# One block of V combined a slot sooner, two weighted sums a slot later, and the raw weight copies moved to GpSimd, in a masked attention layer on one core

## The chip, the cores and the metric

The kernel runs on one core of one Trainium2 chip. The metric is the device time of one execution in microseconds, lower is better. TensorE is called PE here (its weight loads PEld), VectorE DVE, ScalarE ACT, GpSimd POOL and SyncE SP, as in the profile.

## The reference

128 graphs with 128 nodes of 768 features each, in float32. Twelve heads of 64 features attend over the nodes; the adjacency matrix masks the scores and adds a small bias.

```python
h = jnp.maximum(_layernorm(x, axis=-1), 0.0)
q, k, v = (_split_heads(h @ W + b) for W, b in ((Wq, bq), (Wk, bk), (Wv, bv)))
scores = jnp.einsum('bhqd,bhkd->bhqk', q, k) / jnp.sqrt(HD) + beta * adj_e
scores = jnp.where(adj_e > 0, scores, -9000000000000000.0)
out = jnp.einsum('bhqk,bhkd->bhqd', softmax(scores), v)
return x + out            # heads put side by side again
```

## The kernel before

**Groups and slices.** Four graphs (512 rows) make a group, so there are 32 groups, G = 0 to 31. The projections of a group come in three slices of weight columns: `qk0` (the first half of the columns of Wq and Wk), `v` (all of Wv) and `qk1` (the second half of Wq and Wk), called first, second and third slice. Group 0 is computed plainly (`plain_slice`); while it runs, the weights of the fast scheme below are prepared.

**Products and slots.** From group 1 on, a slice is a matrix product of 3 x 3 blocks worked out by 15 block products in place of 27 (`PRODUCTS`), each of which has again seven inner products in place of eight. One block product is one slot: `product_z` issues 28 matmuls on PE (L540). The left operands are blocks A of the activation and sums S of them (`SUMS_A`, DVE, L454); the right ones are blocks B of the weights and sums T of them, kept in DRAM and loaded again in each group, five ahead (`load_T`, L329), or resident in SBUF. The products add up in PSUM along four chains; `uses` says after which product a chain's value enters which result block (r, j), and with what sign: the first time a copy on ACT or DVE (L553 to L561), later an add on DVE (L564).

**What sets the order.** From group 0's second slice on, the order of instructions is the one written out in the program (`manual_schedule`): each engine works through its instructions in this order, and `todo` lists say in which slot a task is issued. In `run`, a slot issues the matmuls of its product, then `behind_product` (masks of the scores of the slot before, the tasks of this slot, what has been put off until now), then the uses of the product, then the trailing ACT work, then the tasks marked "post". Group 0's first slice stands ahead of that and is ordered by the scheduler of the tile framework.

**Combining a block.** When a result block has its last use, `later(decode, lag)` puts its combination on POOL off by `lag` slots: 1 as a rule; `LAG` (L118) has 4 slots for the product with the index 8 (V's block (1,0)) and 5 for the one with the index 12 (V's block (0,0)). The second slice ends with these two products, at its slots 13 and 14, so their combinations are issued in slots 2 and 4 of the third slice. For V, `decode` is five POOL instructions (L591 to L595), which write a tile v that the weighted sums read; for Q and K it is four (L580 to L583).

**Scores and weighted sums.** `scores` (L617) multiplies Q by K for a pair of heads in all four graphs; it reads the combined blocks (0, j) for its first two graphs and (1, j) for the other two. DVE adds the bias and the mask (L625), ACT takes the exponential (L627). `attend` (L657) puts a weighted sum of V into the list `between`; its 16 matmuls (L670) are then issued in the slot after the one named, two behind each inner product of that slot. Then ACT copies the result out of PSUM (L679), DVE takes the reciprocals of the row sums (L640, L641), ACT scales eight blocks (L653), DVE adds x (L686) and SP stores (L690). `attention` (L959) issues, for a slot n, the load of x for that block in slot n - 3 (L604) and the weighted sum behind slot n. The third slice of group G has the weighted sums of the first half of the heads: pair 2 behind slot 3 (it reads V's blocks (0,1) and (1,1)), pair 1 behind slot 8 and pair 0 behind slot 11 (both read (0,0) and (1,0)). The first slice of group G + 1 has the scores of the second half of the heads, behind its slots 1, 3 and 5.

**Activations of the next group.** In slots 1 and 4 of the third slice, `turn_act` turns blocks A10 and A12 of the next group (DVE, L449) and makes their inner sums on POOL (`inner`, L459 to L461); `sum_acts` makes five of the sums S in slots 6 to 10, and two more in slots 0 and 1 of the next slice (S7, S0).

**Preparing the weights.** `prepare` gives steps that run during group 0. `sums` makes a sum T of weight blocks (DVE, L294 and L296). `finish` fills the seven zones of a block: for a sum the four raw quarters are there already; for one of the raw blocks B01, B21 and B22, three copies of 128 x 128 on ACT (L306) put three of them into place. `rest` then makes two zones on DVE (L276, L277) and two on POOL (L278, L279), and SP writes the block to DRAM (L282) unless it is resident. Three raw blocks in three slices make nine. The blocks live in a ring of five tiles, so a sixth waits until the first has been written out.

Of the kernel before, what the change touches and what calls it, by code (L numbers as in the profile page):

```python
# [114 lines left out]


SPOT = ("S7", "S0", "S5", "S14", "S11", "S6", "S1", "S9", "S10", "S2")
LAG = {("v", 8): 4, ("v", 12): 5}  # L118
ZONES = (5, 1, 2, 3, 4, 0, 6)
LEFT = (6, 2, 1, 4, 3, 5, 0)  # L120
RIGHT = (3, 4, 2, 0, 1, 5, 6)
# [4 lines left out]
def direct(ctx, tc, x, adj, wq, bq, wk, bk, wv, bv, beta, out, bad):  # L126
# [10 lines left out]
    nc = tc.nc  # L137
# [55 lines left out]
    for g in range(2):  # L193
        t = xg[0, g]
# [69 lines left out]
    def quarters(t):  # L264
        return t[:, 0:6].rearrange("p (c z) n -> p c z n", c=2)[:, :, 0:2]

    def prepare(sl):

        def home(name):
            n = [i for i, p in enumerate(PRODUCTS) if p[1] == name][0]  # L270
            if (sl, n) in resident:
                return resident[sl, n]
            return work.tile([P, 7, P], F32, tag="T", name=f"prep_{sl}_{n}", bufs=RING)

        def rest(n, t, b11, b12, b22):
            nc.vector.tensor_tensor(t[:, 6], b12, b11, ALU.subtract)  # L276
            nc.vector.tensor_tensor(t[:, 2], b22, b12, ALU.add)  # L277
            nc.gpsimd.tensor_tensor(t[:, 4], t[:, 1], t[:, 6], ALU.add)  # L278
            nc.gpsimd.tensor_tensor(t[:, 5], t[:, 0], t[:, 4], ALU.subtract)  # L279
            if (sl, n) not in resident:  # L280
                k = kept[sl, n] = dram.tile([P, 7, P], F32, name=f"kept_{sl}_{n}")
                nc.sync.dma_start(k, t)  # L282

        made = {}

        def sums(name):
            for out, a, b, sign in SUMS_B:
                if out == name:
                    if out not in made:
                        made[out] = home(out)  # L290
                    at = [quarters(made[q]) if q in made else wt[sl, q] for q in (a.strip("-"), b)]
                    op = ALU.add if sign > 0 else ALU.subtract
                    if a[0] == "-":
                        nc.vector.scalar_tensor_tensor(quarters(made[out]), at[0], -1.0, at[1], op0=ALU.mult, op1=op)  # L294
                    else:
                        nc.vector.tensor_tensor(quarters(made[out]), at[0], at[1], op)  # L296

        def finish(name):
            n = [i for i, p in enumerate(PRODUCTS) if p[1] == name][0]
            if name in made:  # L300
                t = made[name]
                rest(n, t, t[:, 3], t[:, 4], t[:, 1])
            else:
                t, b = home(name), wt[sl, name]
                for z, c, i in ((3, 1, 0), (0, 0, 0), (1, 0, 1)):
                    nc.scalar.copy(t[:, z], b[:, c, i])  # L306
                rest(n, t, b[:, 1, 0], b[:, 1, 1], b[:, 0, 1])

        steps = []
        for first, then_finish in PREPARED:  # L310
            for name in first:
                steps.append(lambda name=name: sums(name))
            for name in then_finish:
                steps.append(lambda name=name: finish(name))
        return steps
# [175 lines left out]
    def later(f, slots=1):  # L491
        while len(deferred) < slots:
            deferred.append([])
        deferred[slots - 1].append(f)
# [29 lines left out]
    def product_z(G, sl, n):  # L524
# [21 lines left out]
        for (r, j), sign in uses:  # L546
# [19 lines left out]
            if not left[key]:  # L566
                later(lambda r=r, j=j: decode(G, sl, r, j), LAG.get((sl, n), 1))
        if n == mine[-1]:
# [3 lines left out]
    def decode(G, sl, r, j, e=nc.gpsimd):  # L572

        t = qk[G, sl, r, j]

        def twice(z):
            return t[:, z:z + 1].to_broadcast([P, 2, P])

        if sl != "v":
            e.tensor_tensor(t[:, 1:4:2], t[:, 1:4:2], twice(5), ALU.add)  # L580
            e.tensor_tensor(t[:, 2:5:2], t[:, 2:5:2], twice(1), ALU.add)  # L581
            e.tensor_tensor(t[:, 4], t[:, 4], t[:, 6], ALU.add)  # L582
            e.tensor_tensor(t[:, 0:7:6], t[:, 0:7:6], twice(2), ALU.add)  # L583
            return
        v = vt[G, sl, r, j] = vring[nv[0] % len(vring)]
        nv[0] += 1

        def heads(z):
            return t[:, z].rearrange("p (h d) -> p h d", d=HD)

        e.tensor_tensor(v[:, 0:2, 0:HD], heads(5), heads(3), ALU.add)  # L591
        e.tensor_tensor(t[:, 1], t[:, 1], t[:, 5], ALU.add)  # L592
        e.tensor_tensor(t[:, 2:5:2], t[:, 2:5:2], twice(1), ALU.add)
        e.tensor_tensor(v[:, 2:4, 0:HD], heads(4), heads(6), ALU.add)  # L594
        e.tensor_tensor(v[:, 4:8, 0:HD].rearrange("p (z h) d -> p z h d", z=2),  # L595
                        t[:, 0:7:6].rearrange("p z (h d) -> p z h d", d=HD),
                        heads(2)[:, None].to_broadcast([P, 2, 2, HD]), ALU.add)
        leave(G, sl, r, j)
# [184 lines left out]
    def slice_z(G, sl, todo):  # L783
        run([product_z(G, sl, n) for n in order_of(G, sl)], todo)
# [163 lines left out]
    def then(at, f, *args):  # L948
        todo.setdefault(at, []).append(lambda: f(*args))
# [9 lines left out]
    def attention(G, u, at):  # L959
        for n, j in at:  # L960
            then(n - 3, load_xo, G, 3 * u + j)
            then((n, "post"), attend, G, 3 * u + j, 5)
# [6 lines left out]
    def turn_act(G, slots):  # L969
        for at, name in slots:  # L970
            then(at, to_hT, G, int(name[1]), int(name[2]))
            then(at, inner, G, name)

    def sums_at(G, slots):
        for at, name in slots:
            then(at, sum_acts, G, name)
# [50 lines left out]
    for G in range(1, NG):  # L1027
        more = G + 1 < NG
        todo.clear()
        then(1, scores, G - 1, 1, 2)  # L1030
        then(3, scores, G - 1, 1, 0)
        then((5, "post"), scores, G - 1, 1, 1)
        attention(G - 1, 1, ((7, 2), (10, 0), (12, 1)))
        if G == 1:
            sums_at(1, ((0, "S6"), (1, "S7"), (2, "S0"), (5, "S5"), (7, "S14"), (9, "S11")))
            then((0, "post"), load_x, 2, 0)
            for n, at in enumerate((0, 0, 0, 3, 4, 5, 6, 7)):
                then((at, "post"), load_half, 2, n)
            for n, at in enumerate((3, 4, 5, 6, 7, 8, 9, 10)):
                then(at, half_stats, 2, n)  # L1040
            then(10, row_moments, 2, 3, 5)
        else:
            sums_at(G, ((0, "S7"), (1, "S0"), (4, "S5"), (7, "S14"), (9, "S11")))
            if more:
                for g in range(2):
                    for h in range(2):
                        then((2 * g + h, "post"), norm, G + 1, g, 2 * h, 2 * h + 2)
                turn_act(G + 1, ((5, "A01"), (6, "A00"), (11, "A02")))
                then((12, "post"), load_x, G + 1, 1)
        slice_z(G, "qk0", todo)  # L1050

        todo.clear()
        then(0, scores, G, 0, 2)
        then(2, scores, G, 0, 1)
        then(7, scores, G, 0, 0)
        if more:
            then((11, "post"), add_raw, G + 1)
            if G == 1:
                for g in range(2):
                    then((2 + g, "post"), norm, 2, g)  # L1060
                turn_act(2, ((5, "A01"), (6, "A00"), (7, "A02"), (14, "A11")))
                then((8, "post"), load_x, 2, 1)
                for g in range(2, GRP):
                    then((10 + g, "post"), norm, 2, g)
            else:
                for n, at in enumerate((5, 6, 8, 9)):
                    then((at, "post"), norm, G + 1, 2 + n // 2, n % 2 * 2, n % 2 * 2 + 2)
                turn_act(G + 1, ((12, "A11"),))
            if G + 2 < NG:
                for n, at in enumerate((0, 0, 0, 3, 5, 6, 8, 9)):  # L1070
                    then((at, "post"), load_half, G + 2, n)
                for n, at in enumerate((3, 5, 6, 8, 9, 11, 12, 13)):
                    then(at, half_stats, G + 2, n)
        slice_z(G, "v", todo)

        todo.clear()
        if not more:
            break
        attention(G, 0, ((3, 2), (8, 1), (11, 0)))
        turn_act(G + 1, ((1, "A10"), (4, "A12")))  # L1080
        sums_at(G + 1, ((6, "S1"), (7, "S9"), (8, "S2"), (9, "S6"), (10, "S10")))
        bias(G + 1, 0, 2, 4, 5)
        if G + 2 < NG:
            then(5, row_moments, G + 2)
            then((6, "post"), load_x, G + 2, 0)
        slice_z(G, "qk1", todo)
# [151 lines left out]
```

## Time and profile before

| | |
|---|---|
| median of 3 runs | 2921.13 us (2919.94 to 2922.12) |
| the profiled execution | 2921.16 us |
| its span, first to last instruction | 2919.4 us |
| mean granted PE clock | 0.966 |
| PE, DVE, ACT, POOL busy | 94%, 80%, 52%, 74% |
| DMA moved, mean | 707.01 MB, 242 GB/s |

The profile gives the busy time of each engine as a share of the span. Its waits say which group of instructions stood idle for which other, summed over the run, with the number of times and the longest. A timeline row has the start in us from the span's start, the duration, the engine, the line of the kernel and the tiles written and read; in square brackets stands the idle time ahead of the row and what ended it. A busy PE is not PE at its peak. The granted clock is a share of full speed.

### The profile page before, as it was taken

What the parts mean: (1) busy time and instruction counts of PE and PEld (TensorE: products, weight loads), DVE (VectorE), ACT (ScalarE), POOL (GpSimd) and SP (SyncE); (2) the same over time, 40 slices, a digit from 0 to 9 for tenths busy, and PEclk for the clock granted to TensorE, in tenths of its full rate; (3) what the DMA queues carried; (4) which work ended last, traced back from release to release, by engine and by line L of the source; (5) the groups of instructions that cost most, each with busy time, mean ns of one, the idle gap of its engine ahead of it and who ended that gap; (6) DMA issues with size and microseconds to landing.
All of it is one profiled execution on the core that took longest, in us unless ns stands there. A gap on an engine that the chain in (4) does not pass through costs nothing.

```text
span 2919.4 us, 121277 instructions
## 1 busy us (share of the span) xinstructions
PE 2750.8 (94%) x52029; PEld 2631.6 (90%) x52029; DVE 2343.6 (80%) x3212; ACT 1504.3 (52%) x3818; POOL 2170.9 (74%) x3152
## 2 busy tenths in 40 slices
PE   8899999999999999999999999999999999999998
PEld 7589999999989998999999999999899899999997
DVE  3888888888887878887888888888788788888775
ACT  2255554555554555554555545555545555555544
POOL 2757877777787778787777777787877787777775
PEclk9899999999999999999999999999999999999999
DMA  6698888888888888788888888887888888888775
GB/s 155 219 278 262 232 249 252 261 251 240 232 253 251 260 242 241 235 255 254 257 242 230 255 249 263 247 240 234 248 256 258 242 235 244 256 257 255 225 212 160
DMA packets 543010, 707.01 MB, mean 242 GB/s; under 512 B 107388, under 2 KB 406152, under 8 KB 542472
## 3 DMA queue, kind: packets, MB, share of 16 engines
q1 hardware_dynamic: 541312, 698.45, 80.5%
q8 instruction: 411, 6.73, 0.9%
q10 hardware_dynamic: 1160, 0.79, 0.1%
q14 instruction: 127, 1.04, 0.1%
HBM read 633.51 MB, written 65.59 MB: 239 GB/s over the span
## 4 chain that ended last, share of the span: by engine, by line
PE 71%; POOL 14%; DVE 7%; issue 1%; DMA 1%; ACT 1%; DVEq 0%; POOLq 0%; SPq 0%; ACTq 0%
PE pair L540 59%; PE pair L617 6%; PE pair L670 5%; DVE home L564 2%; POOL v L594 2%; POOL A L460 1%; POOL v L591 1%; POOL A L461 1%; POOL home L583 1%; POOL home L582 1%; DMA sbig<-in_x_dram 1%; POOL A L459 1%; POOL home L581 1%; POOL v L595 1%; POOL home L592 1%
## 5 line engine op out<-in xcount | busy, mean ns | idle before, releaser
L564 DVE TENSOR_TENSOR home<-home,pair 128x896 f32<-128x896 f32 x798 | 847.9, 1071 | 332.3 <-PE pair L540 299.1
L540 PE MATMUL pair<-sbig,T_qk 128*64 128x128 f32 x14756 | 1013.6, 280 | 7.1 <-DMA T_qk<-kept_qk 3.7
L540 PEld LDWEIGHTS pair<-sbig,T_qk 128*64 128x64 f32 x14756 | 820.6, 141 | 24.7 <-issue 18.9
L670 PE MATMUL pair<-v,e 128*64 128x65 f32 x6048 | 429.2, 234 | 119.4 <-POOL v L594 118.8
L653 ACT ACTIVATE e<-e,sm 128x64 f32<-128x64 f32 x1512 | 382.4, 336 | 251.7 <-DVE sm L641 250.5
L670 PEld LDWEIGHTS pair<-v,e 128*64 128x64 f32 x6048 | 389.2, 149 | 132.5 <-POOL v L594 126.0
L540 PE MATMUL pair<-T_v,sbig 128*64 128x128 f32 x7812 | 456.1, 273 | 1.5 <-issue 0.9
L540 PEld LDWEIGHTS pair<-T_v,sbig 128*64 128x64 f32 x7812 | 430.4, 137 | 8.3 <-issue 6.2
L558 ACT ACTIVATE home<-pair 128x640 f32<-128x640 f32 x319 | 223.8, 701 | 278.7 <-PE pair L540 276.0
L580 POOL TENSOR_TENSOR home<-home 128x256 f32<-128x256 f32 x319 | 268.1, 841 | 98.6 <-DVE home L564 95.1
L679 ACT COPY e<-pair 128x520 f32<-128x520 f32 x189 | 111.1, 588 | 435.0 <-PE pair L670 435.0
L540 PE MATMUL pair<-A,T_qk 128*64 128x128 f32 x4340 | 310.1, 273 | 1.7 <-DVE home L564 1.7
L583 POOL TENSOR_TENSOR home<-home 128x256 f32<-128x256 f32 x319 | 255.2, 800 | 25.0
L581 POOL TENSOR_TENSOR home<-home 128x256 f32<-128x256 f32 x319 | 255.2, 800 | 25.0
L540 PE MATMUL pair<-A,res_qk 128*64 128x128 f32 x4340 | 264.1, 273 | 1.2 <-ACT home L560 1.2
L459 POOL TENSOR_TENSOR A<-A 128x256 f32<-128x256 f32 x186 | 137.9, 742 | 159.3 <-DVE A L449 154.2
L591 POOL TENSOR_TENSOR v<-home 128x128 f32<-128x128 f32 x160 | 98.6, 616 | 205.6 <-DVE home L564 205.6
L627 ACT ACTIVATE e<-e 128x1024 f32<-128x1024 f32 x189 | 199.9, 1058 | 97.1 <-DVE e L625 96.7
L540 PEld LDWEIGHTS pair<-A,res_qk 128*64 128x64 f32 x4340 | 240.5, 137 | 1.7 <-ACT home L560 1.7
L438 ACT ACTIVATE x<-x,block 128x192 f32<-128x192 f32 x480 | 234.4, 541 | 5.0 <-DMA x<-in_x_dram 5.0
L540 PEld LDWEIGHTS pair<-A,T_qk 128*64 128x64 f32 x4340 | 234.6, 137 | 2.1 <-DVE home L564 1.9
L625 DVE SCALAR_TENSOR_TENSOR e<-pair,biasT 128x1024 f32<-128x1024 f32 x189 | 227.3, 1202 | 4.9 <-PE pair L617 1.5
(182 smaller groups left out, 4639.8 us busy)
## 6 DMA issues: line engine op xcount, KB each, us to landing
T_qk<-kept_qk SPq DMA_DIRECT2D x682, 448.0 KB
T_v<-kept_v SPq DMA_DIRECT2D x341, 448.0 KB
xo<-in_x_dram SPq DMA_DIRECT2D x189, 256.0 KB
out_dram<-xo SPq DMA_DIRECT2D x189, 256.0 KB
x<-in_x_dram SPq DMA_DIRECT2D x248, 192.0 KB
sbig<-in_x_dram SPq DMA_DIRECT2D x186, 192.0 KB
half<-in_x_dram SPq DMA_DIRECT2D x60, 192.0 KB
kept_qk<-prep_qk SPq DMA_DIRECT2D x22, 448.0 KB
```

The costliest lines, as they stand in the source:

```text
L438: nc.scalar.activation(t, t, AF.Relu, bias=shift[G, n], scale=rstd[G, n])
L540: nc.tensor.matmul(p[q:q + HD, at, :], lhs[:, q:q + HD], rhs, start=(first and at % 4 == 0), stop=True, skip_group_check=True)
L558: nc.scalar.activation(t[:, 0:5], p[:, 0:5], AF.Copy, scale=float(sign))
L564: nc.vector.tensor_tensor(t, t, p[:, 0:7], op)
L580: e.tensor_tensor(t[:, 1:4:2], t[:, 1:4:2], twice(5), ALU.add)
L581: e.tensor_tensor(t[:, 2:5:2], t[:, 2:5:2], twice(1), ALU.add)
L583: e.tensor_tensor(t[:, 0:7:6], t[:, 0:7:6], twice(2), ALU.add)
L617: nc.tensor.matmul(ps[k:k + HD, i, g * N:(g + 1) * N], keys[r, k:k + HD], queries[r], start=True, stop=True)
L625: nc.vector.scalar_tensor_tensor(e, ps, SCORE_CAP * ISCALE, bias, op0=ALU.min, op1=ALU.add)
L627: trailing.append(lambda: nc.scalar.activation(e, e, AF.Exp, scale=1.0 / ISCALE))
L653: nc.scalar.activation(o[:, r, b, 0:HD], pa[:, r, b, 0:HD], AF.Copy, scale=t[:, 1, r, b:b + 1])
L670: nc.tensor.matmul(pa[q:q + HD, 2 * g + i, :], k[:, q:q + HD], vt[G, "v", r, h // 4][:, 4 * g + h % 4, :], start=True, stop=True, skip_gro ...
```

## The change

Three edits. V's block (0,0) is put off by 4 slots in place of 5, so its combination is issued in slot 3 of the third slice, ahead of the inner sums of A12 (slot 4). The weighted sums of head pairs 1 and 0 go behind slots 9 and 12 in place of 8 and 11, that is, into slots 10 and 13; their loads of x go from slots 5 and 8 to slots 6 and 9. This holds for groups 1 to 30; group 31 has only the first of the two edits. And the raw weight blocks are copied by two POOL instructions (128 x 256 and 128 x 128) in `rest`, between the DVE instructions and POOL's own sums, in place of three ACT copies ahead of them.

```diff
-LAG = {("v", 8): 4, ("v", 12): 5}
+LAG = {("v", 8): 4, ("v", 12): 4}
...
-        def rest(n, t, b11, b12, b22):
+        def rest(n, t, b11, b12, b22, b=None):
             nc.vector.tensor_tensor(t[:, 6], b12, b11, ALU.subtract)
             nc.vector.tensor_tensor(t[:, 2], b22, b12, ALU.add)
+            if b is not None:
+                nc.gpsimd.tensor_copy(t[:, 0:2], b[:, 0])
+                nc.gpsimd.tensor_copy(t[:, 3], b[:, 1, 0])
             nc.gpsimd.tensor_tensor(t[:, 4], t[:, 1], t[:, 6], ALU.add)
             nc.gpsimd.tensor_tensor(t[:, 5], t[:, 0], t[:, 4], ALU.subtract)
...
                 t, b = home(name), wt[sl, name]
-                for z, c, i in ((3, 1, 0), (0, 0, 0), (1, 0, 1)):
-                    nc.scalar.copy(t[:, z], b[:, c, i])
-                rest(n, t, b[:, 1, 0], b[:, 1, 1], b[:, 0, 1])
+                rest(n, t, b[:, 1, 0], b[:, 1, 1], b[:, 0, 1], b)
...
-        attention(G, 0, ((3, 2), (8, 1), (11, 0)))
+        attention(G, 0, ((3, 2), (9, 1), (12, 0)))
         turn_act(G + 1, ((1, "A10"), (4, "A12")))
```

## The prediction, made before the changed kernel was run

> **What bounds the kernel now.** I read the page first, then who waited for whom, then the timelines of PE, POOL and DVE over one group of four graphs (all groups repeat the same 45 slots in about 88.7 us).
>
> ```profile
> span 2919.4 us, 121277 instructions
> PE 2750.8 (94%) x52029; PEld 2631.6 (90%) x52029; DVE 2343.6 (80%) x3212; ACT 1504.3 (52%) x3818; POOL 2170.9 (74%) x3152
> PE pair L670 <- POOL v L594: 118.8, 30, 4.1
> ```
>
> PE is busy 94% of the span, and one wait holds nearly all of its idle time: 30 times, once in each of 30 groups, the weighted sum of L670 waits for POOL to combine a block of V (L591 to L595). Over one group, PE's own timeline (start, duration, engine, line) reads:
>
> ```profile
> 1818.36 1.92 PE L540 MATMUL pair<-sbig,T_qk 128*64 128x128 f32 x32
> 1824.35 0.70 PE L670 MATMUL pair<-v,e 128*64 128x65 f32 x8 [4.07 <-POOL v L594]
> ...
> 1830.80 1.69 PE L540 MATMUL pair<-A,T_qk 128*64 128x128 f32 x28
> 1832.33 0.38 PE L540 MATMUL pair<-sbig,T_qk 128*64 128x128 f32 x4
> ...
> 1834.79 1.70 PE L540 MATMUL pair<-A,T_qk 128*64 128x128 f32 x28
> ...
> 1837.85 3.22 PE L540 MATMUL pair<-sbig,T_qk 128*64 128x128 f32 x56
> 1841.00 1.10 PE L617 MATMUL pair<-home 64*64 64x128 f32 x32
> ```
>
> Slot 9 of the third slice stands still for 4.07 us. A slot with a weighted sum takes 2.46 us (1832.33 to 1834.79), a plain one 1.53 (1830.80 to 1832.33). From 1824.35 to 1830.80, though, the two slots behind the stall take 6.45 instead of 3.99. The view by stretches (length; busy time and count of PE, PEld, DVE, ACT, POOL; granted clock; DMA share; GB/s) says why:
>
> ```profile
> 1824.30:1830.80 6.50, 6.46 (x85) 6.46 (x86) 1.96 (x2) 0.59 (x1) 5.22 (x8) 0.57 0.63 162
> ```
>
> The granted clock is 0.57 there: PE comes back at about half clock, which costs another 6.45 - 3.99 = 2.46 us. The stall is thus 6.53 us of a group, and 30 of them 196 us: that is what seems to be on offer. Whether it can be had is decided by POOL (the name before the arrow is written; L591 opens a combination of V, L580 one of Q and K, L459 the inner sums of an activation):
>
> ```profile
> 1801.47 0.47 POOL L591 TENSOR_TENSOR v<-home 128x128 f32<-128x128 f32 x1 [3.79 <-DVE home L564]
> ...
> 1816.84 0.73 POOL L459 TENSOR_TENSOR A<-A 128x256 f32<-128x256 f32 x1
> ...
> 1820.07 1.30 POOL L591 TENSOR_TENSOR v<-home 128x128 f32<-128x128 f32 x1
> ...
> 1823.11 1.18 POOL L594 TENSOR_TENSOR v<-home 128x128 f32<-128x128 f32 x1
> ...
> 1830.00 1.51 POOL L580 TENSOR_TENSOR home<-home 128x256 f32<-128x256 f32 x1 [0.96 <-DVE home L564]
> ...
> 1834.00 0.73 POOL L580 TENSOR_TENSOR home<-home 128x256 f32<-128x256 f32 x1 [0.33 <-DVE home L564]
> ...
> 1839.32 0.73 POOL L583 TENSOR_TENSOR home<-home 128x256 f32<-128x256 f32 x1
> 1840.01 1.57 POOL L580 TENSOR_TENSOR sbig<-sbig 128x256 f32<-128x256 f32 x1
> 1841.66 1.46 POOL L581 TENSOR_TENSOR sbig<-sbig 128x256 f32<-128x256 f32 x1
> ```
>
> From 1801.47 to beyond 1841 POOL waits for nobody but for 0.96 and 0.33 us: it works off a backlog. The first scores of the next slice (L617 at 1841.00) need what it ends at 1840.05 (L583 at 1839.32). So PE's stall in slot 9 is one face of a POOL that is late until 1840; take the stall away and PE meets the same POOL 16 us later.
>
> **The change part by part: the third slice.** V's block (0,0) (five POOL instructions) goes ahead of the inner sums of A12 (three, from 1816.84). It starts at 1816.84 instead of 1820.07. In before it took 3.04 us up to L594; so L594 starts about 1819.9 and ends about 1821.1 at its stretched 1.18 us. The sum that reads it moves from slot 9 to slot 10. Slot 8 starts at 1818.36, so slot 10 starts at 1821.42 and its first sum some 0.2 later: no stall, or one of some tenths while L595 ends. What moves with it costs nothing: per weighted sum 16 matmuls, one PSUM copy and eight scalings on ACT, two small DVE instructions and one add, a load and a store on SP, all one slot later. The loads go behind one weight load each on SP; the last add goes behind the first masking of the next slice on DVE. ACT is busy 52% and the buffers have the same number of slots between uses. The A12 sums end near 1825, about when DVE comes to the sum that reads them (slot 10); were they late by a microsecond, DVE would still be ahead of POOL's backlog.
>
> What is late next: without stall and half clock PE reaches the scores 6.53 us sooner, at 1834.47. POOL has the same work, five instructions of it ahead of three; its two waits (0.96 + 0.33) vanish, as DVE's products come sooner, so its L583 would end at 1840.05 - 1.29 = 1838.76. Against that stand two DVE sums:
>
> ```profile
> 1839.34 1.66 DVE L454 TENSOR_TENSOR sbig<-A,sbig 128x896 f32<-128x896 f32 x1
> 1840.92 1.61 DVE L454 TENSOR_TENSOR sbig<-sbig 128x896 f32<-128x896 f32 x1
> ```
>
> While they run, POOL's L580 and L581 take 1.57 and 1.46 where 0.73 is usual: 0.84 + 0.73 us. In before they begin 1.49 us after PE has left the slice (1837.85) and hit the block behind the one that PE waits for. With PE 6.5 us sooner they begin near 1833 to 1834, and hit the block that PE waits for, or the one ahead of it. So L583 ends between 1838.76 (no hit) and 1840.33 (both hit); I take 1840.2, as POOL is busy without a gap there. The first half of the scores needs only an older block and is done before; the second half, at 1841.00 + 0.52 = 1841.52 in before (half of the 32 matmuls of that row), starts at 1840.2: **1.3 us sooner**. But PE has then stood still for some 5 us (half of the scores done by 1835), longer than the 4.07 that cost it the clock, and the 2.46 us at half clock now come behind POOL's release, where nothing hides them; in before they ran in the shadow of POOL's backlog. A group becomes 2.46 - 1.3 = **1.15 us longer**; 30 groups, **+34 us**. Both ends: 2.46 - 2.76 = -0.3 (sums hit nothing; -9 us) and 3.4 - 1.2 = +2.2 (all work up to 1848 at half clock; +66 us).
>
> **The raw blocks.** In before ScalarE makes 27 copies (three for each of nine blocks, 0.70 us for three in the row below). Three of them sit in its queue behind a copy of V that PE delivers late:
>
> ```profile
> 67.97 0.70 ACT L306 COPY prep_qk<-sbig 128x128 f32<-128x128 f32 x3
> POOL prep_qk L278 <- ACT prep_qk L306: 23.7, 1, 23.7
> DVE prep_qk L296 <- POOL prep_qk L279: 18.7, 1, 18.7
> PE pair L365 <- DVE st L354: 9.8, 1, 9.8
> 70.20:80.00 9.80, 0.04 (x1) 0.00 (x0) 7.69 (x24) 0.00 (x0) 6.36 (x13) 0.59 0.69 280
> 80.00:96.00 16.00, 14.45 (x50) 11.43 (x51) 15.69 (x36) 2.59 (x8) 8.91 (x16) 0.72 0.75 240
> 103.00:141.00 38.00, 37.61 (x481) 25.75 (x480) 32.46 (x60) 18.07 (x42) 28.98 (x52) 1.00 0.54 192
> ```
>
> POOL waits 23.7 us for them, DVE 18.7 behind POOL, and PE 9.8 behind DVE; then PE has 16 us at a clock of 0.72 (4.5 us lost). With the copies on POOL, right ahead of its own sums, this chain goes: 9.8 + 4.5 = 14.3 us at most. A POOL copy isn't in the trace; the nearest rows are POOL's sums of the same sizes (busy us in all, then mean ns of one):
>
> ```profile
> L580 POOL TENSOR_TENSOR home<-home 128x256 f32<-128x256 f32 x319 | 268.1, 841 | 98.6 <-DVE home L564 95.1 <-DVE sm L640 2.9 <-issue 0.7
> L582 POOL TENSOR_TENSOR home<-home 128x128 f32<-128x128 f32 x319 | 187.7, 589 | 25.0
> ```
>
> Nine pairs at 0.84 + 0.59 are 13 us (from nothing up to 1.57 + 1.19 each, 25 us), of which the six pairs behind 54 us (8.6 us) fall on a POOL that idles 16 us in the last two stretches shown (7.1 of 16, 9.0 of 38). I charge 2.3 us for those that meet no idle time, and take **-12 us** (0 to -14).
>
> Sum against the profiled execution's 2921.16 us (span 2919.4, and 1.8 around it; the median of the runs is 2921.13): 2921.2 + 34 - 12 = **2943 us**.
>
> **The rivals.** (a) *POOL's release comes early enough.* Same chain, but the two sums hit nothing that PE waits for: L583 at 1838.76, -0.3 us a group: 2921 - 9 - 12 = 2900. It decides at 1841.52 - 2.46 = 1839.06: any release before that makes the group shorter. For it: the sums' place is mine, not the trace's. Against: POOL has no gap in which they could run free. (b) *The clock stays up.* If the scores' two halves split the idle time, or POOL is early by 2 us, PE keeps full clock: -1.3 us a group, 2921 - 39 - 12 = 2870. Against: the stall of 4.07 us shown above lowered it. The Trainium skill ("TensorE: Matmul & The Clock Gate", What's actually happening) has the clock halved after one idle window of about 3.4 us and restored after one busy one; the 4.07 us stall and the 0.57 row agree, and by it a stall under 3.4 would be this rival. (c) *POOL isn't the bound*: the stall goes and nothing takes its place: 2921 - 196 - 12 = 2713. Against it: POOL's 40 us without a gap. (d) *Copies and sums on POOL get in DVE's way*, as L580 at 1.57 shows: nine pairs at 1.57 + 1.19 use up the first part's gain: 2943 + 12 = 2955, and with +2.2 a group up to 2987. The Trainium skill ("SBUF — State Buffer", Who interferes with whom) has VectorE with two SBUF inputs and GpSimd exclude each other, while ScalarE has ports of its own; that speaks against moving copies to GpSimd. (e) *The change doesn't do what it says*: L594 still ends behind PE in slot 10 (my margin is 0.5 us). PE would then stall there a little and less at the scores: the same release, the same 2943.
>
> **How the numbers follow.** Forecast with (e): 0.48, 2925 to 2965. (a) 0.20, (b) 0.10, (c) 0.05, (d) 0.17. The range leaves out (c), the lower half of (b) and the far end of (d): 2870 to 2975. About 0.2% (5.8 us) is what a measurement of this kernel can tell from no change. Faster: (b), (c) and 0.16 of (a), together 0.31. Within 0.2%: 0.04 of (a) and 0.08 of the forecast's near end, 0.12. Slower: the other 0.40 of the forecast and (d), 0.57.
>
> **What would show it.** Right: L670's wait for L594 falls from 118.8 us to under 20; a wait of L617 for POOL L583 of about 4 to 5 us in each of 30 groups, at slot 1 of the first slice; 0.50 clock right behind it; POOL without a gap from the same L591 to that L583; no 23.7 us wait of L278 and no 9.8 us wait of L365. Wrong: PE without a wait over 1 us in a group, DVE's L454 pair away from POOL's work, or a clock of 1.00 behind the scores.

## The result, and the profile after

The changed kernel takes 2902.89 us (median of 4 runs, 2898.48 to 2905.51) against 2921.62 us of the kernel before (4 runs, 2919.94 to 2923.01): a ratio of 0.9935, 95% interval 0.9917 to 0.9952. It is 19 us faster, where 22 us slower was predicted. The profiled execution took 2902.2 us (span 2900.4). From L308 on, line numbers are one higher in the changed kernel: L618 is the L617 of before.

The page of the changed kernel and its waits (engine, tile and line that waited, what for; us in total, times, longest):

```profile
span 2900.4 us, 121318 instructions
PE 2753.9 (95%) x52029; PEld 2621.5 (90%) x52029; DVE 2325.4 (80%) x3212; ACT 1497.1 (52%) x3791; POOL 2157.1 (74%) x3170
```

```profile
PE pair L618 <- POOL home L583: 85.3, 26, 3.5
PE pair L618 <- POOL sbig L583: 13.6, 4, 3.4
PE pair L671 <- POOL v L596: 8.2, 27, 0.3
```

The 118.8 us that the weighted sums waited have become 8.2; 98.9 us of waiting have come up at the scores, once in each of 30 groups. The wait has moved, as predicted, and is a little shorter. PE's timeline over the same group as in the prediction (it lies 17.24 us sooner here: POOL's row of 1801.47 is now at 1784.23):

```profile
1817.38 0.67 PE L618 MATMUL pair<-home 64*64 64x128 f32 x16
1821.44 1.51 PE L618 MATMUL pair<-home 64*64 64x128 f32 x16 [3.40 <-POOL home L583]
1822.88 3.26 PE L541 MATMUL pair<-sbig,T_qk 128*64 128x128 f32 x28
1825.92 2.22 PE L541 MATMUL pair<-sbig,res_qk 128*64 128x128 f32 x28
1828.07 0.67 PE L618 MATMUL pair<-sbig 64*64 64x128 f32 x16
```

PE does the first half of the scores, stands 3.40 us for POOL, and then needs 1.51 us for the second half, where the first took 0.67 (x16 counts records, two for each matmul). The view by stretches has the clock (length; busy time and count of PE, PEld, DVE, ACT, POOL; granted clock; DMA share; GB/s):

```profile
1821.40:1825.90 4.50, 4.36 (x44) 3.63 (x46) 1.82 (x2) 1.62 (x3) 4.20 (x6) 0.50 0.16 48
```

POOL's own timeline up to the release:

```profile
1784.23 0.47 POOL L592 TENSOR_TENSOR v<-home 128x128 f32<-128x128 f32 x1 [3.78 <-DVE home L565]
...
1799.61 0.46 POOL L592 TENSOR_TENSOR v<-home 128x128 f32<-128x128 f32 x1
...
1802.96 1.18 POOL L595 TENSOR_TENSOR v<-home 128x128 f32<-128x128 f32 x1
...
1807.73 1.02 POOL L424 TENSOR_TENSOR row<-verow,nhalf 128x4 f32<-128x4 f32 x1
...
1816.65 1.19 POOL L583 TENSOR_TENSOR home<-home 128x128 f32<-128x128 f32 x1
1817.92 1.45 POOL L584 TENSOR_TENSOR home<-home 128x256 f32<-128x256 f32 x1
...
1820.93 0.46 POOL L583 TENSOR_TENSOR home<-home 128x128 f32<-128x128 f32 x1
1821.46 0.73 POOL L584 TENSOR_TENSOR home<-home 128x256 f32<-128x256 f32 x1
```

From 1784.23 to the release POOL has no idle row. The release is the third of the four instructions of the fourth combination: L583 ends at 1821.39, PE starts at 1821.44. DVE's side of the same stretch:

```profile
1807.84 1.08 DVE L455 TENSOR_TENSOR sbig<-A,A 128x896 f32<-128x896 f32 x1
...
1816.21 1.31 DVE L455 TENSOR_TENSOR sbig<-A,sbig 128x896 f32<-128x896 f32 x1
1817.44 1.34 DVE L455 TENSOR_TENSOR sbig<-sbig 128x896 f32<-128x896 f32 x1
```

The last two are the sums S7 and S0. POOL's L583 and L584 beside them take 1.19 and 1.45 us, one combination ahead of the one that PE waits for; experiment 7 shows that the sums stretch them.

The other gain lies in group 0. The 23.7 us wait of L278 and PE's 9.8 us wait of L365 are gone, and PE runs through the same stretches at full clock:

```profile
70.20:80.00 9.80, 9.80 (x50) 8.09 (x51) 9.60 (x21) 1.31 (x2) 7.13 (x16) 1.00 1.00 323
80.00:96.00 16.00, 16.00 (x156) 11.37 (x156) 11.35 (x30) 8.81 (x20) 12.54 (x18) 1.00 0.78 210
```

Compared at the same PE instruction (own reading of the two traces), the changed kernel is level at 67 us, 11.2 us ahead at 82.7 us of before's time, 15.8 ahead at 95.7, and 16.0 ahead at 145.7, where group 1 begins. So 16 of the 19 us come from group 0, and some 3 us from 30 groups.

### The profile page after: what moved, and what is told of

It is laid out like the page before. It is cut to its first block, busy times and chain, and to the rows that moved or that the text cites. A ratio compares the mean times of both kernels' runs of the same rounds, so it can differ in the third digit from the quotient of the medians.

```text
span 2900.4 us, 121318 instructions
## 1 busy us (share of the span) xinstructions
PE 2753.9 (95%) x52029; PEld 2621.5 (90%) x52029; DVE 2325.4 (80%) x3212; ACT 1497.1 (52%) x3791; POOL 2157.1 (74%) x3170
## 4 chain that ended last, share of the span: by engine, by line
POOL 57%; PE 23%; issue 12%; DVE 4%; ACT 0%; POOLq 0%; DMA 0%; SPq 0%; ACTq 0%; DVEq 0%
PE pair L541 19%; POOL home L584 7%; POOL home L582 6%; POOL home L581 6%; POOL home L583 5%; POOL v L596 5%; POOL home L594 5%; POOL v L595 4%; POOL A L461 3%; POOL home L593 3%; POOL A L460 3%; PE pair L618 3%; POOL v L592 3%; DVE home L565 2%; POOL A L462 2%
## 5 line engine op out<-in xcount | busy, mean ns | idle before, releaser
L541 PE MATMUL pair<-sbig,T_qk 128*64 128x128 f32 x14756 | 961.5, 281 | 7.6 <-DMA T_qk<-kept_qk 4.0
L541 PEld LDWEIGHTS pair<-sbig,T_qk 128*64 128x64 f32 x14756 | 841.4, 142 | 28.3 <-issue 24.5
L671 PE MATMUL pair<-v,e 128*64 128x65 f32 x6048 | 402.9, 222 | 8.9 <-POOL v L596 8.2
L671 PEld LDWEIGHTS pair<-v,e 128*64 128x64 f32 x6048 | 357.8, 137 | 19.9 <-POOL v L596 15.5
L626 DVE SCALAR_TENSOR_TENSOR e<-pair,biasT 128x1024 f32<-128x1024 f32 x189 | 228.0, 1206 | 145.0 <-PE pair L618 141.9
L541 PE MATMUL pair<-A,T_qk 128*64 128x128 f32 x4340 | 333.5, 273 | 0.3 <-DVE home L565 0.2
L584 POOL TENSOR_TENSOR home<-home 128x256 f32<-128x256 f32 x319 | 279.5, 876 | 25.0
L618 PE MATMUL pair<-home 64*64 64x128 f32 x5216 | 209.2, 285 | 91.9 <-POOL home L583 85.3
L581 POOL TENSOR_TENSOR home<-home 128x256 f32<-128x256 f32 x319 | 235.6, 739 | 74.0 <-DVE home L565 70.3
L618 PEld LDWEIGHTS pair<-home 64*64 64x64 f32 x5216 | 144.2, 136 | 141.2 <-POOL home L583 95.0
L582 POOL TENSOR_TENSOR home<-home 128x256 f32<-128x256 f32 x319 | 237.0, 743 | 25.0
```

The source lines that it names most:

```text
L541: nc.tensor.matmul(p[q:q + HD, at, :], lhs[:, q:q + HD], rhs, start=(first and at % 4 == 0), stop=True, skip_group_check=True)
L618: nc.tensor.matmul(ps[k:k + HD, i, g * N:(g + 1) * N], keys[r, k:k + HD], queries[r], start=True, stop=True)
L626: nc.vector.scalar_tensor_tensor(e, ps, SCORE_CAP * ISCALE, bias, op0=ALU.min, op1=ALU.add)
L671: nc.tensor.matmul(pa[q:q + HD, 2 * g + i, :], k[:, q:q + HD], vt[G, "v", r, h // 4][:, 4 * g + h % 4, :], start=True, stop=True, skip_gro ...
```

## The experiments

The theory after the result: (T) in a group PE is held by one run of POOL work that ends with the release of the first scores; the slots only choose where PE stands still, and the half clock that follows the stall decides the rest. So the slot edits bring next to nothing, and the copies all. Rivals: (R1) the slot edits bring the gain and the copies are neutral; (R2) the stall at the scores has a cause of its own that a single move would lift; (R3) another chain holds the groups, and the half clock is hidden under it.

**1. The copies alone.** The changed kernel with the two slot edits undone.

```diff
-LAG = {("v", 8): 4, ("v", 12): 4}
+LAG = {("v", 8): 4, ("v", 12): 5}
...
-        attention(G, 0, ((3, 2), (9, 1), (12, 0)))
+        attention(G, 0, ((3, 2), (8, 1), (11, 0)))
```

> The copies on GpSimd alone; the block of V and the weighted sums stay as before. Theory (the copies free a chain of waits in the first 150 us, and the third slice's edits only move PE's stall): 2921.6 - 15.8 = 2906 us, PE's wait for the combination of V at 118 us as before. Rival (the gain comes from the third slice, the copies are hidden): 2921 us.

Measured: 2906.06 us (2904.24 to 2907.49), ratio to before 0.9947 (0.9931 to 0.9964). The copies alone are worth 16 us. R1 falls.

**2. The slots alone.** The kernel before with the slot edits and ACT's copies kept.

```diff
-LAG = {("v", 8): 4, ("v", 12): 5}
+LAG = {("v", 8): 4, ("v", 12): 4}
...
-        attention(G, 0, ((3, 2), (8, 1), (11, 0)))
+        attention(G, 0, ((3, 2), (9, 1), (12, 0)))
```

> The third slice's two edits alone; the copies stay on ScalarE. Theory: about 0.1 us a group, 2918 us, with PE's wait of some 3.4 us a group at the first scores and GpSimd still waiting 23.7 us for ScalarE's copies. Rival (the gain comes from the third slice): 2903 us.

Measured: 2919.20 us (2913.16 to 2925.85, 10 runs), ratio 0.9994 (0.9984 to 1.0004): no change that can be measured, although every group's 4 us stall is gone from slot 9. Its waits show the same wait at the scores (line numbers of before):

```profile
PE pair L617 <- POOL home L582: 87.4, 26, 3.6
PE pair L617 <- POOL sbig L582: 13.4, 4, 3.4
```

**3. The block sooner, the weighted sums in their old slots.** The changed kernel with one slot edit undone.

```diff
-        attention(G, 0, ((3, 2), (9, 1), (12, 0)))
+        attention(G, 0, ((3, 2), (8, 1), (11, 0)))
```

> The changed kernel with the weighted sums back behind slots 8 and 11; only the block of V is sooner. Theory (GpSimd sets when the scores can run; what the move gains is paid back because the stall of 3.4 us halves the clock): the stall splits into about 1.3 us at the weighted sum and 2.1 us at the scores, both too short to lower the clock (2.6 us did not, 2.8 us did), so 29 groups keep about 2.9 us each: 2903 - 84 = 2819 us. Rival (the clock is beside the point, GpSimd gives the pace of the next slice too): 2903 us within 5.

Measured: 2921.47 us (2910.82 to 2930.57, 10 runs), ratio 0.9993 (0.9983 to 1.0002). Both expectations missed: it is slower than the changed kernel. The waits of PE:

```profile
PE pair L618 <- POOL home L583: 67.9, 26, 2.9
PE pair L671 <- POOL v L595: 36.4, 29, 1.8
```

The idle time is split in two, but neither part got short enough for the clock: by the clock records (own reading), each of the 24 stalls of 2.3 to 2.9 us in groups 2 to 30 still has half clock in it or right behind it. And POOL's run to the release, from the block of V that stands first in the timeline above (1784.23), takes 38.1 us in the median of 27 groups against 37.2 in the changed kernel (own reading). The instructions are the same, and POOL has no idle row there; so they are stretched more, by which of DVE's was not followed up.

**4. The weighted sums later, the block in its old slot.** The other slot edit undone.

```diff
-LAG = {("v", 8): 4, ("v", 12): 4}
+LAG = {("v", 8): 4, ("v", 12): 5}
```

> The changed kernel with V's block (0,0) combined in slot 4 as before; only the weighted sums are later. Theory: about 2.7 us of stall at the weighted sum in slot 10 and 0.9 us at the scores. 2.7 us lies at the edge (2.6 us kept the clock, 2.8 us lowered it): between 2819 us (clock kept in all groups) and 2903 us (lowered in all). Rival (the clock is beside the point): 2903 us within 5, wherever the stall lies.

Measured: 2891.46 us (2883.07 to 2898.14), ratio 0.9903 (0.9885 to 0.9922), between the two expectations and 11 us better than the changed kernel. Its waits:

```profile
PE pair L671 <- POOL v L595: 72.9, 29, 2.6
PE pair L618 <- POOL home L583: 14.2, 7, 2.0
```

With experiments 1 and 3 this makes a square, all with POOL's copies: neither slot edit 2906.1, the block sooner 2921.5 (+15.4), the sums later 2891.5 (-14.6), both 2902.9 (-3.2). The two slot edits work against each other: the sums a slot later bring 15 to 19 us, the block a slot sooner costs 11 to 15. That each does so much alone is not what (T) says; only their sum is next to nothing. In the profiled runs (own reading; order as above) PE worked at half clock for 143, 124, 102 and 146 us, half of which is lost, and idled for 126, 144, 115 and 117 us between 150 and 2780 us. So the sums alone save half clock and idle time, and the block alone saves some half clock but adds idle time; the sizes do not add up to the medians.

**5. TensorE kept at work through the stall.** In each group 88 extra matmuls between the two halves of the first scores, into a part of the PSUM tile that the second half overwrites.

```diff
+FILL = 88
...
+            if u == 1 and j == 2 and g == 1:
+                for n in range(FILL):
+                    i, k = n % 2, n // 2 % 2 * HD
+                    r = slice(i * HD, (i + 1) * HD)
+                    nc.tensor.matmul(ps[k:k + HD, i, 2 * N:3 * N], keys[r, k:k + HD], queries[r],
+                                     start=True, stop=True)
```

> The changed kernel with 88 more matmuls of 64 x 128 (about 2.8 us at full clock) in the first scores of the first slice, between their halves, into a region that the real ones overwrite: PE computes while it would wait, and nothing else changes. Theory (the stall of 3.4 us halves the clock, and that costs some 0.9 + 1.2 + 0.4 us in slots 1, 2 and 3 of the first slice): those 2.5 us a group come back, 2903 - 29 x 2.5 = 2830 us, the clock stays at 1.00. Rival (GpSimd gives the pace of the whole slice, the clock is hidden): 2903 us within 5, in spite of a full clock.

Measured: 2915.76 us (2907.78 to 2922.94, 10 runs), ratio 0.9976 (0.9962 to 0.9990); the clock is 0.996. The clock stayed up, and nothing was gained: by this run alone R3 would stand. But PE's timeline of a group (x176 is two records for each of the 88; lines 1 or 7 higher than in the changed kernel) shows that the fill was too long:

```profile
1830.45 4.98 PE L625 MATMUL pair<-home 64*64 64x128 f32 x176
1835.26 0.60 PE L619 MATMUL pair<-home 64*64 64x128 f32 x10
1836.92 0.44 PE L619 MATMUL pair<-home 64*64 64x128 f32 x6 [1.06 <-issue]
```

POOL's release of this group:

```profile
1833.53 0.46 POOL L584 TENSOR_TENSOR home<-home 128x128 f32<-128x128 f32 x1
```

It ended at 1833.99; the fill holds PE until 1835.43. It cost 1.44 us itself, and about a microsecond of idle time that no other engine ended follows in some groups. So it was run again, shorter.

**6. The same with 56 matmuls.**

```diff
-FILL = 88
+FILL = 56
```

> The changed kernel with 56 extra matmuls in every group between the two halves of the first scores (their results are overwritten; the work is added, nothing is left out); the run with 88 of them took 4.98 us for them in the group where the release came 3.4 us after the first half, and so held TensorE 1.44 us past the release, with idle time of about a microsecond behind it in some groups. 56 take 56/88 x 4.98 = 3.2 us, which ends 0.2 us ahead of the release. Theory (each group of the changed kernel pays 3.4 us of waiting and about 2.5 us of half clock behind it; the first fill removed the half clock and gave it back by its own length): 2915.8 less 30 groups x 1.4 to 2.2 us = 2850 to 2875 us, clock above 0.99. Rival (the time is held by another chain, GpSimd's or VectorE's, and the half clock is hidden under it): 2900 to 2916 us again, with the clock above 0.99.

Measured: 2853.95 us (2847.32 to 2855.80), ratio 0.9769 (0.9752 to 0.9785), as the theory had it; R3 falls. The timeline, with POOL's release:

```profile
1787.63 0.67 PE L619 MATMUL pair<-home 64*64 64x128 f32 x16
1788.12 3.24 PE L625 MATMUL pair<-home 64*64 64x128 f32 x112
1791.18 0.62 PE L619 MATMUL pair<-home 64*64 64x128 f32 x16
...
1794.93 0.67 PE L619 MATMUL pair<-sbig 64*64 64x128 f32 x16
```

```profile
1789.87 0.46 POOL L584 TENSOR_TENSOR home<-home 128x128 f32<-128x128 f32 x1
```

From the second half of the scores to the next scores are 3.75 us (1791.18 to 1794.93), against 6.63 in the changed kernel (1821.44 to 1828.07). But in this group the fill still holds PE 0.85 us past the release, which came at 1790.33. Where PE starts at the release itself, the stretch takes 4.39 us at full clock: in 18 of 27 groups here, and in the two groups of the changed kernel that kept the clock (own reading of PE's start times). The reason is in `decode` and `scores`: the third quarter of the scores reads what the third instruction of the combination completes, the last quarter what the fourth writes, 0.80 us later. So the half clock costs 6.63 - 4.39 = 2.24 us in the group shown for the changed kernel, and 1.9 us in the mean of 27 groups (6.22 against 4.33). Over all of it, 49 us by the medians, 1.6 us for each of 30 groups.

**7. DVE's two sums moved.** S7 and S0 from slots 0 and 1 of the first slice to slots 2 and 3, so that they no longer meet POOL's combinations ahead of the release.

```diff
-            sums_at(G, ((0, "S7"), (1, "S0"), (4, "S5"), (7, "S14"), (9, "S11")))
+            sums_at(G, ((2, "S7"), (3, "S0"), (4, "S5"), (7, "S14"), (9, "S11")))
```

> The changed kernel with the two VectorE sums S7 and S0 in slots 2 and 3 of the first slice in place of 0 and 1. In the changed kernel they stretch two GpSimd instructions ahead of the release from 0.46 to 1.19 and from 0.73 to 1.45 us. Theory (VectorE's sums and GpSimd's hold each other up, and this delays PE): the release comes 1.4 us sooner, the stall falls from 3.4 to about 2 us, 1 to 3 us a group: 2815 to 2873 us. Rival (the stretching costs nothing that PE waits for): 2903 us.

Measured: 2874.88 us (2864.95 to 2884.20), ratio 0.9817 (0.9787 to 0.9847): 28 us better than the changed kernel, 2 us short of the weak end of what the theory gave.

```profile
PE pair L618 <- POOL home L583: 66.1, 26, 2.8
```

The wait went from 85.3 to 66.1 us, 0.74 us for each of 26 groups: what one sum had added to a POOL instruction, not two. DVE's and POOL's timelines say why:

```profile
1804.98 1.31 DVE L455 TENSOR_TENSOR sbig<-A,sbig 128x896 f32<-128x896 f32 x1
1811.06 1.23 DVE L626 SCALAR_TENSOR_TENSOR e<-pair,biasT 128x1024 f32<-128x1024 f32 x1 [4.77 <-PE pair L618]
...
1815.30 1.15 DVE L455 TENSOR_TENSOR sbig<-sbig 128x896 f32<-128x896 f32 x1
```

```profile
1805.42 1.19 POOL L583 TENSOR_TENSOR home<-home 128x128 f32<-128x128 f32 x1
1806.68 0.72 POOL L584 TENSOR_TENSOR home<-home 128x256 f32<-128x256 f32 x1
```

S7 (from a block A) still stands ahead of the mask of L626 in DVE's queue, runs at once and stretches L583 to 1.19; only S0 has gone behind the mask, and L584 is back at 0.72.

**8. The order on POOL.** In the changed kernel, the combination of block (0,1) of the third slice is put behind those that the first scores read (in all groups but the last).

```diff
-LAG = {("v", 8): 4, ("v", 12): 4}
+LAG = {("v", 8): 4, ("v", 12): 4, ("qk1", 11): 4}
...
-                later(lambda r=r, j=j: decode(G, sl, r, j), LAG.get((sl, n), 1))
+                later(lambda r=r, j=j: decode(G, sl, r, j), LAG.get((sl, n), 1) if G < NG - 1 or sl == "v" else 1)
```

> The changed kernel with the combination of Q's and K's block (0,1) put off from slot 12 of the third slice to slot 0 of the next, so that GpSimd combines the blocks in the order in which the scores read them: (1,2) third in place of fourth, (0,0) fourth, (0,1) fifth. Theory (only GpSimd's release of the first scores holds PE up): the release comes one combination, about 3 us, sooner, PE waits 0 to 0.5 us at the first scores and about 1 us at the third, the clock stays up: 4 to 5 us a group, 2760 to 2790 us. Rival (GpSimd's total work gives the pace): the stall turns up at the next scores, 2880 to 2903 us.

Measured: 2801.46 us (2796.67 to 2808.95), ratio 0.9572 (0.9552 to 0.9592), clock 0.996. 101 us go with one move; that is the theory's side, though 11 us short of its range. What is left of the stalls at the scores:

```profile
PE pair L618 <- POOL home L584: 33.2, 49, 1.1
PE pair L618 <- POOL home L583: 9.0, 25, 1.0
```

**9. The same order with the old slots.** Experiment 1 with the same order.

```diff
-LAG = {("v", 8): 4, ("v", 12): 5}
+LAG = {("v", 8): 4, ("v", 12): 5, ("qk1", 11): 4}
```

(and the second line of experiment 8)

> As the run before (blocks combined in the order in which the scores read them), but V's block and the weighted sums in the slots of the kernel before. Theory: the stall of 4 us at the weighted sum in slot 9 stays and hides GpSimd's backlog, so the order alone brings nothing: 2906 us as with the copies alone. Rival (the order is what matters, wherever the weighted sums stand): 2760 to 2790 us.

Measured: 2905.83 us (2903.42 to 2908.07), ratio 0.9936 (0.9917 to 0.9955): nothing beside experiment 1's 2906.06.

```profile
PE pair L671 <- POOL v L595: 120.5, 30, 4.3
```

PE still stands in slot 9 for V, so a release that comes sooner finds nobody waiting. Slots alone -3 us, order alone 0, both -105: each edit removes one of two waits that stand one behind the other. So R2 holds only in part: a single move on POOL lifts the stall at the scores, and is worth something only where PE no longer stands in slot 9.

**10. Order and sums together.** Experiments 7 and 8 in one.

> The run that put the decode of block (0,1) behind (0,0)'s combinations (2801.5 us), with the two weighted sums S7 and S0 two slots later as well (alone worth 28 us, 2874.9 against 2902.9). Theory (what is left of the wait at the first scores, 3.98 against 2.66 us in that slot, is the two GpSimd instructions that the sums stretch by about 0.7 us each): that slot falls to about 2.7 us and 30 groups x 1.0 to 1.3 us go, 2762 to 2772 us. Rival (the sums now meet other GpSimd instructions, those of the delayed combination, or PE waits for the fifth combination instead): 2790 to 2805 us.

Measured: 2796.77 us (2795.27 to 2804.70), ratio 0.9580 (0.9562 to 0.9598): not to be told from experiment 8. The first scores' slot fell from 3.98 to 3.18 us in the mean of groups 4 to 30 (own reading of PE's start times), but the third scores' slot grew from 3.81 to 4.50: the rival. The sums now meet the combinations that these scores wait for:

```profile
1762.97 0.67 PE L618 MATMUL pair<-home 64*64 64x128 f32 x16
1764.67 0.45 PE L618 MATMUL pair<-home 64*64 64x128 f32 x8 [1.04 <-POOL home L583]
```

Experiments 8 and 10 are the best versions: 4.2 to 4.3% below the kernel before, and 3.5 to 3.7% below the changed one (2801.46 and 2796.77 by 2902.89). The new order with the sums later and the block in its old slot, which experiment 4 suggests, was not run.

## Why the prediction was wrong, point by point

**The stall in slot 9 goes: right.** The weighted sum's longest wait is 0.3 us; the block's L595 (L594 before) ends at 1804.14, that is 1821.38 in before's time, where about 1821.1 was said.

**PE reaches the scores sooner: right.** 1817.38 + 17.24 = 1834.62, said was 1834.47.

**PE meets the same POOL, stands still, and the clock drops: right in kind.** The stall is 3.40 us where some 5 were said. Experiment 2, without the copies, shows the whole of it: the stall of 4 us goes, the wait at the scores comes, and the time stays.

**"I take 1840.2, as POOL is busy without a gap there": this step failed.** The release came at 1821.39 + 17.24 = 1838.63, 1.57 us sooner than that. The two sums did hit POOL as forecast, by 0.73 and 0.72 us. Two other things were missed. In before, the sum S10 meets POOL's L580 of 1830.00 and stretches it to 1.51 us, 0.78 more than usual. Its row on DVE's timeline of before:

```profile
1829.84 1.09 DVE L454 TENSOR_TENSOR sbig<-A,A 128x896 f32<-128x896 f32 x1
```

In the changed kernel that sum runs at 1807.84 and meets POOL's L424, which takes 1.02 us, no more than the same instruction in before, where no sum meets it:

```profile
1824.93 1.02 POOL L423 TENSOR_TENSOR row<-verow,nhalf 128x4 f32<-128x4 f32 x1
```

So the 0.78 us go. And the second half of the scores starts at the third instruction of the combination, not the fourth: all 30 long waits name L583, the L582 of before. Its row there:

```profile
1838.78 0.46 POOL L582 TENSOR_TENSOR home<-home 128x128 f32<-128x128 f32 x1
```

It ended at 1839.24, 0.81 us ahead of the L583 taken (1840.05). 1840.2 - 0.78 - 0.81 = 1838.61. So the term "1.3 us sooner" was mis-sized: it was 2.84 (1841.52 - 1838.68, PE's start in before's time).

**2.46 us at half clock: near.** 2.24 us in this group and 1.9 in the mean by experiment 6. The prediction left out 0.67 us beside it: the last quarter of the scores now follows right behind the release, and waits for the fourth instruction. In before the stretch from the second half to the next scores took 3.72 us (1841.52 to this row), at full clock behind a release it takes 4.39:

```profile
1845.24 0.67 PE L617 MATMUL pair<-sbig 64*64 64x128 f32 x16
```

**The sum of a group.** 2.46 - 1.3 = +1.15 was predicted; (6.63 - 3.72) - 2.84 = 2.91 - 2.84 = +0.07 in this group came. Over the run the slots are worth -3.2 us beside experiment 1 and -3.2 beside the before of experiment 2, about -0.1 us a group, where +34 us were charged. It lies in the bound that the prediction gave (-0.3 to +2.2): the wrong end was chosen, and the sign of the forecast hung on it. With a price of 0 the forecast would have been 2909. Of the 40 us between the forecast and the result, some 37 lie here and 4 in the copies.

**The copies: right in kind, too small.** -12 was said, with 14.3 as the most; -16 came. Two of the changed kernel's POOL rows for the copies (busy us in all, mean ns of one):

```profile
L279 POOL COPY prep_qk<-sbig 128x256 f32<-128x256 f32 x3 | 1.3, 418 | 0.4 <-DMA kept_qk<-prep_qk 0.4
L280 POOL COPY prep_qk<-sbig 128x128 f32<-128x128 f32 x3 | 1.5, 492 | 0.0
```

Over all rows the larger copy takes 0.42 to 0.63 us in the mean and the smaller 0.29 to 0.49, where POOL's sums of these sizes (0.84 and 0.59) had been taken; the 18 copies are 7.8 us in place of 13. No run shows the 2.3 us charged for them. And the "most" left out 1.50 us that PE idled at L379 in the same stretch: 9.81 + 1.50 + 4.5 = 15.8.

**The rivals.** (a) gave 2900, for a release ahead of 1839.06; the release came at 1838.63, though not for its reason: the sums hit, and S10 and the third instruction made up for it. That 2900 lies so near to 2902.89 is in part luck: its -9 us for the slots were -3, and the -12 for the copies -16. (b), (c) and (e) did not come. (d) is out: the copies cost less than the sums beside them.

**The signs.** All that were named for the prediction being right came (8.2 us at L671, a stall at the scores, 3.3 us in the mean where 4 to 5 were said, 0.50 clock behind it, POOL without a gap, no 23.7 and 9.8 us waits), and the time still went the other way. They show that the stall moved; none of them says which of the two prices is the larger.

What stays open: why the square of experiments 1, 3 and 4 comes to just these sizes, above all why the block sooner costs 11 to 15 us. That the half clock and the moved meetings of DVE and POOL are its causes is read from the traces; no run holds the one still and varies the other.

## What to carry to other kernels

When the waited-for engine has no idle row up to its next release, moving the waiting work mostly moves the stall; what helped most here was to change what that engine does first together with the move (-3 us for the moves alone, 0 for the order alone, -105 for both). Test each move alone, though: here one of the two brought 15 us, and the other took it back. Price the next release to the instruction: which of its parts the waiter reads, and which meetings with another engine vanish as well as which arise. And where two prices of about 2 us are set against each other 30 times, a choice of 1.5 us in one of them is the sign of the answer; then both ends are the forecast.

## What the runs showed of the hardware that was not expected

Stalls well under 3.4 us lowered the clock. In experiment 7, one of 2.66 us:

```profile
401.70:404.40 2.70, 0.08 (x4) 0.00 (x0) 0.00 (x0) 2.70 (x9) 2.53 (x4) 1.00 0.70 165
404.40:406.40 2.00, 1.60 (x30) 1.19 (x32) 0.64 (x1) 0.73 (x2) 1.86 (x3) 1.00 0.75 256
406.40:409.80 3.40, 3.40 (x36) 3.40 (x34) 2.89 (x4) 1.94 (x3) 3.17 (x5) 0.50 0.20 29
409.80:415.00 5.20, 5.20 (x110) 4.69 (x110) 4.09 (x5) 3.70 (x9) 3.66 (x5) 1.00 0.31 93
```

PE stands until 404.4, works 2 us at full clock, and only then gets half clock for 3.4 us. By the clock records of groups 2 to 30 (own reading), 24 of 27 stalls of 2.3 to 2.9 us in experiment 7 have half clock in them or within 3.5 us behind them, 21 of 29 in experiment 4, and there 8 of 9 of 1.5 to 2.3 us; the two of 2.3 to 2.9 us in the changed kernel have none. The Trainium skill ("TensorE: Matmul & The Clock Gate", What's actually happening) has one idle window of about 3.4 us as the condition. These runs differ: less than a whole window was enough in most cases, so rival (b)'s "a stall under 3.4" would not have been enough to keep the clock up.

The clock records of all twelve traces (own reading) say which stalls do it. Within a run the granted clock changes only on a grid of 3.41 us: every spell of half clock that ends within a run is one to four such windows long (173 are one, 91 two). Between 150 and 2780 us, 205 windows at full clock have 2.0 us or more of PE's idle time in them, and 203 of these are followed by a window at half clock; of 65 with 1.6 to 2.0 us, 22 are; of 8650 with less, one is. In the example above the window from 402.99 to 406.41 has 1.8 us of the idle time. So in these runs more than about half a window decided, and a stall of 2.66 us lowers the clock or not by where an edge of the grid cuts it. Experiment 8, whose longest stall at the scores is 1.1 us, ran at 0.996.
